# STU filters of a two-layer network: the lower left quarter of the Toeplitz matrix from three block products, and one product for the even and the odd lags of the same source tokens

## The chip, the cores and the metric

The kernel runs on one core of one Trainium2 chip. The metric is the device time of that core in microseconds (us), from the first to the last instruction of one execution of the whole program. The kernel before takes 2966.78 us (median of three runs, 2966.41 to 2967.76). The engines are named as in the profile: PE is TensorE's matrix multiply, PEld its weight load, DVE is VectorE, ACT is ScalarE, POOL is GpSimd, SP the engine that issues most DMAs.

## The reference, cut to what matters

The input is x (8 images, 128 channels, 32 x 32 positions, fp32). Layer 0 is multi-head attention along rows and then a spectral filter unit (STU); layer 1 is a deformable 1 x 3 convolution and a mixture of experts. Each part has a normalisation ahead of it and a residual sum around it. The change is in the STU, whose tokens are the 1024 positions of an image:

```python
Vf = jnp.fft.rfft(phi, n=n, axis=0)                     # 16 filters
Uf_p = jnp.fft.rfft(u, n=n, axis=1)
Uf_m = jnp.fft.rfft(u * sgn3, n=n, axis=1)              # signs + - + - ...
U_plus = jnp.fft.irfft(Vf[None, :, :, None] * Uf_p[:, :, None, :], n=n, axis=1)[:, :sl]
U_minus = jnp.fft.irfft(Vf[None, :, :, None] * Uf_m[:, :, None, :], n=n, axis=1)[:, :sl]
U_minus = U_minus * sgn[None, :, None, None]
out = jnp.einsum('btkd,k,kde->bte', U_plus, s, Mpp)
out = out + jnp.einsum('btkd,k,kde->bte', U_minus, s, Mpm)
```

This is a causal convolution of the tokens u with each of 16 filters, once plain and once with alternating signs, followed by a 128 x 128 matrix for each filter and sign, summed over the filters. The unit is run on the first 1024, 512, 256 and 128 tokens with four sets of matrices, and the four results are mixed with the weights of a softmax. Three more matrices M_u act on the tokens at lags 0, 1 and 2.

## The kernel before

**Even and odd lags.** The sum and the difference of the plain and the signed convolution are the even and the odd lags of the filter. So the kernel splits the tokens into even and odd ones (parity, 512 of each). An output parity gets the even lags from source tokens of the same parity (term 0) and the odd lags from the other parity (term 1). Each of these is a lower triangular Toeplitz matrix of 512 x 512. A filter lies in SBUF as one tile `teto` of 128 partitions: row p holds the filter reversed and shifted, so that any 128 columns of it are one 128 x 128 Toeplitz block. `read_filter` (L1179) loads it with two DMAs, even lags and odd lags.

**One pass.** The images go in four pairs; the list of work is (pair, filter), 4 x 16 = 64 passes. For a pass, `filter_image` (L1367) is called for each of four (parity, term) and each of two images: four matmuls, whose weights are the four token tiles of 128 tokens and whose moving operands are 512, 384, 256 and 128 columns of the filter, add into one PSUM bank `pu` (128 channels x 512 tokens), and ScalarE copies it to `us` (L1378). fp32 products appear as two records each in the profile. `pu` has two banks in rotation. `mix` (L1380) multiplies the `us` of the pass before, for both images, with this filter's mixing matrices `mf`, in four column ranges (SPANS: 64, 64, 128 and 256 tokens, since the four lengths of the STU end at different tokens), and adds into four PSUM banks `po` that stay open for the whole pair. `start_sums` (L1335) opens these banks with the residual and the lags 0 to 2. In program order a filter product of an image (eight records) is followed by half of a mixing step (three short ranges or the long one), and then by other work.

**The other work.** The second layer of the pair before, and the normalisation of the pair to come, are Python generators in a queue `behind`. `advance(2.6)` (L1411) takes steps from it until their costs add up to 2.6; it is called eight times in a pass, after each half of a mixing step. So the order of instructions on each engine is written out by the program. The steps of an image are: transposes, normalisation (`norm_steps`, L779: statistics and scaling on VectorE, Newton steps for the inverse root on GpSimd), a product `p_g` for each tile of 128 tokens, 24 DMAs from SP that write the tables `tab`, offsets, 24 gathers by GpSimd (`fetch`, L1054, three ahead, from a ring of nine buffers `g`) each with four VectorE steps (L1078), a second normalisation, gates, and 16 expert products `p_e` with four VectorE steps each (L1102). The last pair's second layer runs after the spectral stage, two images interleaved.

**Filters and matrices.** At the start of pass n the filter of pass n+2 is loaded (L1436, three buffers), at its end the matrices for pass n+2 (L1460, three buffers). In the first pair `load_matrices` (L1260) loads M_plus and M_minus, GpSimd makes their sum and difference (L1274, L1275), VectorE scales and adds them to `mf` (L1279, L1281), and SP stores `mf` in DRAM (L1284); the other pairs load it from there (L1267). `lags` (L1242) makes `mu` from M_u on VectorE once, before the first pass.

Of the kernel before, what the change touches and what calls it, by code (L numbers as in the profile page):

```python
# [18 lines left out]
P = 128  # L19
B = 8  # L20
C = 128
# [11 lines left out]
PHI_PAD = 127  # L33
PHI_ROW = PHI_PAD + 1 + HT
GROUPS = ((0, 1), (2, 3), (4, 5), (6, 7))
RATE = (2.6, 3.5)
STAGGER = 16


# [361 lines left out]
class BoundedAttention:  # L401
# [6 lines left out]
    def __init__(self, nc, cp):  # L408
        self.nc = nc
        HG, NH = self.HG, self.NH  # L410
        self.xc = cp.tile([P, T], F32, name="xc")
        self.ht = cp.tile([P, NT, C], F32, name="ht")
        self.hk = cp.tile([P, 2 * HT + 2], F32, name="hk")
        self.wq = cp.tile([C, HG, NH, 32], F32, name="wq")
        self.wk = cp.tile([C, HG, NH, 32], F32, name="wk")
        self.wv = cp.tile([C, C], F32, name="wv")
        self.group = cp.tile([P, NG], F32, name="group")
        self.spread = cp.tile([P, 2, P], F32, name="spread")
        self.pick = cp.tile([P, HG, NH, HD], F32, name="pick")
# [381 lines left out]
class DeformAndExperts:  # L801
# [182 lines left out]
    def image(self, b, x2, alone):  # L984
# [69 lines left out]
        def fetch():  # L1054
            if len(fetched) < len(points):
                i, tap = points[len(fetched)]
                if alone:
                    at = idx[:, i, tap : tap + 1]
                else:
                    if tap == 0:  # L1060
                        here.append(sb.tile([P, TAPS], I32, tag="here", name="here", bufs=3))
                        nc.scalar.copy(here[-1], idx[:, i, :])  # L1062
                    at = here[-1][:, tap : tap + 1]
                g = sb.tile([P, 4 * C], F32, tag="g", name="g", bufs=9)
                nc.gpsimd.indirect_dma_start(  # L1065
                    out=g, out_offset=None, in_=rows,
                    in_offset=bass.IndirectOffsetOnAxis(ap=at, axis=0),
                )
                fetched.append(g)
# [106 lines left out]
        yield  # L1176


def read_filter(nc, t, phi_e, phi_o, k):  # L1179
    nc.sync.dma_start(t[:, 0:HT], bass.AP(phi_e.tensor, k * PHI_ROW, [[1, P], [1, HT]]))  # L1180
    nc.sync.dma_start(
        t[:, HT : 2 * HT + 1], bass.AP(phi_o.tensor, k * PHI_ROW, [[1, P], [1, HT + 1]])
    )
    return t[:, 0:HT], t[:, HT : 2 * HT + 1]


class FirstGroup:
# [30 lines left out]
class Spectral:  # L1218
# [4 lines left out]
    def __init__(self, ctx, tc, dram, phi_e, phi_o, M_u, M_plus, M_minus, coef, x1d, back, given):  # L1223
        nc = self.nc = tc.nc
        cp = ctx.enter_context(tc.tile_pool(name="s_const", bufs=1))
        self.sb = ctx.enter_context(tc.tile_pool(name="s_sb", bufs=1))
        self.up = ctx.enter_context(tc.tile_pool(name="s_u", bufs=2, space=PSUM))
        self.op = ctx.enter_context(tc.tile_pool(name="s_o", bufs=1, space=PSUM))
        self.phi_e, self.phi_o, self.x1d, self.back = phi_e, phi_o, x1d, back
        self.M_u, self.M_plus, self.M_minus, self.coef = M_u, M_plus, M_minus, coef  # L1230
# [23 lines left out]
    def load_filter(self, k):  # L1254


        t = self.sb.tile([P, 2 * HT + 1], F32, tag="teto", name="teto", bufs=3)
        return read_filter(self.nc, t, self.phi_e, self.phi_o, k)

    def load_matrices(self, k, first):  # L1260

        nc, sb = self.nc, self.sb
        mf = sb.tile([C, NFR, 2, C], F32, tag="mf", name="mf", bufs=3)
        if not first:
            nc.sync.dma_start(mf, self.mfd[k])  # L1267
            return mf
# [18 lines left out]
    def prepare(self, group):  # L1287

        nc, sb = self.nc, self.sb
        group["x1"], group["ur"] = [], []  # L1290
        for n, b in enumerate(group["images"]):
            x1 = sb.tile([P, NT, C], F32, tag="x1", name="x1", bufs=2)
            nc.gpsimd.indirect_dma_start(
                out=x1.rearrange("p i c -> p (i c)"), out_offset=None,
                in_=self.x1d.rearrange("b p i c -> (b p) (i c)"),
                in_offset=bass.IndirectOffsetOnAxis(ap=self.back[:, b : b + 1], axis=0),
            )
            group["x1"].append(x1)
            if group["number"] % 2:
                group["ur"].append(sb.tile([P, NT, C], F32, tag="ur", name="ur", bufs=2))  # L1300
            else:
                group["ur"].append(self.given.ur[n])
        group["ut"] = sb.tile([C, 2, 2, HT + 1], F32, tag="ut", name="ut")

    def normal(self, group, newton):

        for x1, ur in zip(group["x1"], group["ur"]):
            yield from norm_steps(self.nc, self.sb, x1, ur, 1e-5, newton)

    def channels(self, group, bank):  # L1310

# [52 lines left out]
        )  # L1364
        group["opened"].add(bank)

    def filter_image(self, group, n, par, term, teto, us):  # L1367

        nc = self.nc
        src = par if term == 0 else 1 - par  # L1370
        flt = teto[0] if term == 0 else teto[1][:, par : par + HT]
        pu = self.up.tile([P, HT], F32, tag="u", name="pu")
        for i in range(4):
            nc.tensor.matmul(  # L1374
                pu[:, i * P : HT], group["ur"][n][:, src * 4 + i, :], flt[:, 0 : HT - i * P],
                start=(i == 0), stop=(i == 3),
            )
        nc.scalar.copy(us[:, n, :], pu)  # L1378

    def mix(self, group, par, term, spans, mf, us, last):  # L1380
        for lo, hi, k in spans:
            self.add(
                group, (par, lo // 256), self.span(group, par, lo, hi), mf[:, k - 1, term, :],
                us[:, 0 : len(group["images"]), lo:hi], last and term == 1,
            )

    def finish(self, group):
# [9 lines left out]
def spectral_and_second_layer(tc, spec, layer, weights):  # L1397
    groups = [{"images": im, "number": g} for g, im in enumerate(GROUPS)]
    work = [(g, k) for g in range(len(groups)) for k in range(NF)]
    spec.prepare(groups[0])  # L1400
    filters = {0: spec.given.filter, 1: spec.load_filter(1)}
    matrices = {0: spec.load_matrices(0, True)}
    spec.lags(weights)
    matrices[1] = spec.load_matrices(1, True)


    behind = deque([spec.channels(groups[0], layer.bank), layer.setup()])
# [14 lines left out]
    for n in range(len(work) + 1):  # L1422
# [9 lines left out]
        if now is not None and now[1] == 0 and now[0]:  # L1432
            for _ in starts[now[0]]:
                pass
        if n + 2 < len(work):
            filters[n + 2] = spec.load_filter(work[n + 2][1])  # L1436
        sums = {}
        for i in range(4 if now or before else 0):
            par, term = divmod(i, 2)
            if now is not None:  # L1440
                group = groups[now[0]]
                us = spec.sb.tile([C, 2, HT], F32, tag="us", name="us", bufs=6)
                sums[i] = us
            for m in range(2):
                unit = now is not None and m < len(group["images"])
                if unit:
                    spec.filter_image(group, m, par, term, filters[n], us)
                if before is not None:
                    if before[1] == 0 and i + m == 0:
                        spec.start_sums(groups[before[0]])  # L1450
                    spec.mix(
                        groups[before[0]], par, term, SPANS[0:3] if m == 0 else SPANS[3:4],
                        matrices[n - 1], kept[i], before[1] == NF - 1,
                    )
                if unit:
                    advance(RATE[2 - len(group["images"])])
        if before is not None and before[1] == NF - 1:
            spec.finish(groups[before[0]])
        if n + 2 < len(work):
            matrices[n + 2] = spec.load_matrices(work[n + 2][1], work[n + 2][0] == 0)  # L1460
        kept, before = sums, now
    while behind:
        advance(1)
# [105 lines left out]
```

## Time and profile before

| | |
|---|---|
| median of three runs | 2966.78 us |
| the profiled execution | 2968.47 us, its span 2966.7 us |
| attention, to the first filter product | 0 to 911 us |
| first pair, passes 0 to 15 | 911 to 1331 us |
| second, third and fourth pair | 1331 to 1803, 2275 and 2745 us |
| second layer of the last pair | 2745 to 2967 us |
| filter products in the profile | 4096 records |
| copies `us` (L1378) | 512 of 585 ns |
| combining steps `mf` (L1279, L1281) | 16 of 354 ns and 48 of 485 ns |
| sums and differences `both` (L1274, L1275) | 32 of some 1265 ns |

A row of the timeline holds start, length, engine, line, operation, output and input names, shape and count of one or several like instructions; in brackets stands the idle time of the engine before it and what ended that. A matmul's record lasts longer than the time to the next one's start, since they are pipelined; work on TensorE is therefore counted from start to start. In a table by windows each engine has its busy time and, in brackets, its count of instructions; the granted TensorE clock (1.00 is full), the share of the DMA engines and GB/s end the row.

### The profile page before, as it was taken

Reading aid. Unit: us, or ns where it says so; the run is one execution under the profiler, and the core shown is the slowest. Engines: PE = TensorE matmul, PEld = TensorE weight load, DVE = VectorE, ACT = ScalarE, POOL = GpSimd, SP = SyncE. Lnnn points to the kernel's source line nnn. Section 1 sums busy time; section 2 is a strip of 40 time slices with the busy share of each in tenths; the row PEclk is TensorE's granted clock in tenths of the full one; section 3 lists DMA queues with packets and bytes.
Section 4 is the critical chain, followed back from the end, with each engine's and each line's share of the span. In section 5 each row is a group of like instructions: output and inputs, shape, how many; then the busy total and the mean of one; then the engine's idle time right before and its main releaser. Section 6 shows DMA issues by size and latency. Waiting matters only on the chain.

```text
span 2966.7 us, 45298 instructions
## 1 busy us (share of the span) xinstructions
PE 2759.9 (93%) x18896; PEld 1693.4 (57%) x18896; DVE 1405.6 (47%) x2882; ACT 982.0 (33%) x1246; POOL 976.3 (33%) x977
## 2 busy tenths in 40 slices
PE   7999999999998999999999999999999999999316
PEld 3555555555555666666666666666666666666103
DVE  4888888888882200000432532333333153333586
ACT  4666667676661111112212111221211221221100
POOL 4777777777881211100200301210210030220230
PEclk9999999999998999999999999999999999999658
DMA  1000000000002322221614411521621441530730
GB/s 27 2 16 16 2 16 16 2 16 9 16 16 83 101 64 64 64 61 51 184 39 128 143 35 36 170 82 41 191 64 36 116 135 34 157 99 8 229 112 15
DMA packets 177012, 199.80 MB, mean 67 GB/s; under 512 B 17237, under 2 KB 135189, under 8 KB 176801
## 3 DMA queue, kind: packets, MB, share of 16 engines
q1 hardware_dynamic: 147328, 134.97, 15.3%
q0 software_dynamic: 16800, 55.59, 6.1%
q10 hardware_dynamic: 12672, 6.29, 0.7%
q8 instruction: 150, 2.46, 0.3%
q14 instruction: 62, 0.50, 0.1%
HBM read 128.88 MB, written 67.92 MB: 66 GB/s over the span
## 4 chain that ended last, share of the span: by engine, by line
PE 58%; DVE 6%; DMA 1%; issue 1%; POOL 0%; ACT 0%; SPq 0%; DVEq 0%; POOLq 0%; ACTq 0%
PE pu L1374 35%; PE po L1362 16%; PE p_e L1096 3%; DVE x L1078 2%; PE p_g L1015 1%; DVE x L1102 1%; DMA tab<-gs 1%; PE p_out L1113 0%; PE p_turn L918 0%; PE p_out L1116 0%; PE p_l L1140 0%; DVE st L785 0%; DVE mv L786 0%; PE p_ut L1318 0%; DMA g<-tab,cn_idx 0%
## 5 line engine op out<-in xcount | busy, mean ns | idle before, releaser
L1378 ACT COPY us<-pu 128x512 f32<-128x512 f32 x512 | 299.4, 585 | 1301.1 <-PE pu L1374 1266.9
L620 POOL TENSOR_TENSOR t<-e 128x1024 f32<-128x1024 f32 x256 | 607.9, 2375 | 199.4 <-ACT e L611 199.2
L648 DVE TENSOR_TENSOR e<-e,rb 128x2048 f32<-128x2048 f32 x256 | 570.8, 2279 | 83.6 <-PE rb L641 83.6
L1374 PE MATMUL pu<-teto,ur 128*128 128x512 f32 (+3 forms) x2048 | 594.4, 433 | 0.0
L611 ACT ACTIVATE e<-s 128x2048 f32<-128x2048 f32 x256 | 480.9, 1879 | 253.2 <-PE s L606 251.3
L1374 PEld LDWEIGHTS pu<-teto,ur 128*128 128x128 f32 x2048 | 386.5, 190 | 273.0 <-issue 185.1
L1362 PE MATMUL po<-us,mf 128*128 128x128 f32 (+2 forms) x2048 | 528.1, 381 | 0.0
L606 PE MATMUL s<-q,k 32*128 32x256 f32 x4096 | 296.1, 403 | 14.0 <-ACT e L611 13.2
L658 PE MATMUL av<-e,vt 128*32 128x256 f32 x4096 | 290.0, 391 | 2.9 <-DVE e L648 1.6
L1374 PE MATMUL pu<-teto,xc 128*128 128x512 f32 x992 | 290.5, 436 | 0.0
L1374 PE MATMUL pu<-teto,ht 128*128 128x512 f32 x992 | 287.7, 433 | 0.0
L1065 POOL DMA_INDIRECT g<-tab,here x144 | 137.6, 956 | 447.0 <-ACT here L1062 252.8
L1374 PEld LDWEIGHTS pu<-teto,xc 128*128 128x128 f32 x992 | 189.0, 191 | 153.9 <-issue 114.2
L1362 PEld LDWEIGHTS po<-us,mf 128*128 128x128 f32 x2048 | 270.9, 192 | 4.1 <-issue 3.9
L1078 DVE SCALAR_TENSOR_TENSOR x<-g,w,x 128x128 f32<-128x128 f32 x704 | 250.0, 356 | 43.0 <-DMA g<-tab,here 11.5
L1102 DVE SCALAR_TENSOR_TENSOR x<-p_e,gates,x 128x128 f32<-128x128 f32 x512 | 177.7, 350 | 188.7 <-PE p_e L1096 172.4
L606 PEld LDWEIGHTS s<-q,k 32*128 32x128 f32 x4096 | 186.4, 185 | 136.9 <-ACT e L611 115.7
L1374 PEld LDWEIGHTS pu<-teto,ht 128*128 128x128 f32 x992 | 187.7, 190 | 110.0 <-issue 64.7
L770 POOL TENSOR_SCALAR rs_v<-rs_v 128x8 f32<-128x8 f32 x18 | 4.4, 245 | 711.3 <-DVE rs_b L768 711.3
L658 PEld LDWEIGHTS av<-e,vt 128*32 128x32 f32 x4096 | 101.7, 109 | 141.4 <-issue 85.2
L1096 PE MATMUL p_e<-ew,tc 128*128 128x512 f32 x256 | 133.1, 626 | 15.4 <-DVE x L1102 10.3
L634 DVE RECIPROCAL r<-z 128x256 f32<-128x256 f32 x64 | 112.5, 1757 | 69.0 <-PE z L627 68.8
(237 smaller groups left out, 1829.0 us busy)
## 6 DMA issues: line engine op xcount, KB each, us to landing
tab<-gs SPq DMA_DIRECT2D x168, 256.0 KB
mf<-mfd SPq DMA_DIRECT2D x48, 512.0 KB
teto<-in_phi_o SPq DMA_DIRECT2D x63, 256.5 KB
teto<-in_phi_e SPq DMA_DIRECT2D x63, 256.0 KB
mfd<-mf SPq DMA_DIRECT2D x16, 512.0 KB
tab<-gs ACTq DMA_DIRECT2D x24, 256.0 KB
xc<-in_x SPq DMA_DIRECT2D x8, 512.0 KB
x1d<-xt SPq DMA_DIRECT2D x8, 512.0 KB
```

Of the source, the lines that this page charges most:

```text
L606: nc.tensor.matmul(s[:, j, c, :], img["k"][rows, hg, 2 * r + c, :], q[rows, qc * QU : (qc + 1) * QU], start=True, stop=True,)
L611: nc.scalar.activation(e.rearrange("p j c q -> p (j c q)"), s.rearrange("p j c q -> p (j c q)"), AF.Exp, scale=float(HD) ** -0.5,)
L620: nc.gpsimd.tensor_add(t, e[:, :, 0, :], e[:, :, 1, :])
L648: nc.vector.tensor_tensor(e, e, un["rb"].unsqueeze(2).to_broadcast([P, NH, 2, QU]), ALU.mult)
L658: nc.tensor.matmul(qrt["av"][32 * j : 32 * j + 32, 0:QU], img["v"][:, 2 * r + c, P * hg + 32 * j : P * hg + 32 * j + 32], un["e", r][:, j, ...
L1065: nc.gpsimd.indirect_dma_start(out=g, out_offset=None, in_=rows, in_offset=bass.IndirectOffsetOnAxis(ap=at, axis=0),)
L1078: nc.vector.scalar_tensor_tensor(x3[:, i, :], fetched[n][:, k * C : (k + 1) * C], w[:, i, tap, k : k + 1], (tok if tap + k == 0 else x3)[: ...
L1096: nc.tensor.matmul(pe, tc[:, i * P : (i + 1) * P], self.ew[:, grp * 4 : grp * 4 + 4, :].rearrange("d e c -> d (e c)"), start=True, stop=True,)
L1102: nc.vector.scalar_tensor_tensor(x3[:, i, :], pe[:, k * C : (k + 1) * C], gate[:, i, grp * 4 + k : grp * 4 + k + 1], x3[:, i, :], ALU.mult ...
L1362: self.nc.tensor.matmul(out, lhsT, rhs, start=bank not in group["opened"], stop=last, skip_group_check=True)
L1374: nc.tensor.matmul(pu[:, i * P : HT], group["ur"][n][:, src * 4 + i, :], flt[:, 0 : HT - i * P], start=(i == 0), stop=(i == 3),)
L1378: nc.scalar.copy(us[:, n, :], pu)
```

## The change

A 512 x 512 Toeplitz matrix has four rows and columns of 128 x 128 blocks T0 (diagonal) to T3. The lower left quarter takes tiles 0 and 1 to output blocks 2 and 3 and needs T2 t0 + T1 t1 and T3 t0 + T2 t1. The kernel after forms W = T2 (t0 + t1) once and adds (T1 - T2) t1 and (T3 - T2) t0: three block products for four. The sums t0 + t1 (`add_tiles`) are made by VectorE once for each image and parity, the differences of blocks (`differences`) by GpSimd once for each pass, for the even and the odd lags.

A product now has both kinds of lags in its moving operand, as two halves of the columns, since both act on the same source tokens. So a unit is (image, source parity), four in a pass. It has seven products: W (2 x 128 columns) in the bank `low`; 2 x 256 and three times 256 columns in the bank `high`; 512 and 256 columns in the bank `low` again. ScalarE copies W out of PSUM, VectorE adds W to the high half on its way to `us`, ScalarE copies the low half. Each of the two banks has one buffer.

```diff
-RATE = (2.6, 3.5)
+RATE = 2.6
...
-                g = sb.tile([P, 4 * C], F32, tag="g", name="g", bufs=9)
+                g = sb.tile([P, 4 * C], F32, tag="g", name="g", bufs=7)
...
-        self.up = ctx.enter_context(tc.tile_pool(name="s_u", bufs=2, space=PSUM))
+        self.up = ctx.enter_context(tc.tile_pool(name="s_u", bufs=1, space=PSUM))
...
-        t = self.sb.tile([P, 2 * HT + 1], F32, tag="teto", name="teto", bufs=3)
-        return read_filter(self.nc, t, self.phi_e, self.phi_o, k)
+        return read_filter(
+            self.nc, self.sb.tile([P, FILTER], F32, tag="teto", name="teto", bufs=2),
+            self.phi_e, self.phi_o, k,
+        )
+
+    def differences(self, t):
+        nc = self.nc
+        d = self.sb.tile([P, 5 * DIFF], F32, tag="diff", name="diff", bufs=2)
+        for lags, width in enumerate((P, P + 1)):
+            at = HT * lags
+            nc.gpsimd.tensor_sub(
+                d[:, DIFF * lags : DIFF * lags + 4 * DIFF].rearrange(
+                    "p (two c) -> p two c", two=2
+                )[:, :, 0:width],
+                t[:, at + P : at + 5 * P].rearrange("p (two c) -> p two c", two=2)[:, :, 0:width],
+                t[:, at + 2 * P : at + 2 * P + width].unsqueeze(1).to_broadcast([P, 2, width]),
+            )
+        return d
...
-        mf = sb.tile([C, NFR, 2, C], F32, tag="mf", name="mf", bufs=3)
+        mf = sb.tile([C, NFR, 2, C], F32, tag="mf", name="mf", bufs=2)
...
+        self.add_tiles(group)
+        yield
+
+    def add_tiles(self, group):
+        for ur, both in zip(group["ur"], group["sum"]):
+            halves = ur.rearrange("p (par i) c -> p par i c", par=2)
+            self.nc.vector.tensor_add(both, halves[:, :, 0, :], halves[:, :, 1, :])
...
+        pw = bank("low")[:, :, 0:P]
+        product(pw, group["sum"][n][:, src, :], blocks(2 * P, 3 * P), True, True)
+        w = self.sb.tile([C, 2, P], F32, tag="us_w", name="us_w", bufs=2)
+        nc.scalar.copy(w, pw)
+        tile = [ur[:, src * 4 + i, :] for i in range(4)]
+        high = bank("high")
+        product(high, tile[2], blocks(0, 2 * P), True)
+        product(high[:, :, 0:P], tile[1], less(0))
+        product(high[:, :, P:], tile[0], less(1))
+        product(high[:, :, P:], tile[3], blocks(0, P), False, True)
+        nc.vector.tensor_tensor(
+            us[:, :, n, 2 * P :].rearrange("c two (b t) -> c two b t", b=2),
+            high.rearrange("c two (b t) -> c two b t", b=2),
+            w.unsqueeze(2).to_broadcast([C, 2, 2, P]), ALU.add,
+        )
+        low = bank("low")
+        product(low, tile[0], blocks(0, 2 * P), True)
+        product(low[:, :, P:], tile[1], blocks(0, P), False, True)
+        nc.scalar.copy(us[:, :, n, 0 : 2 * P], low)
...
+    less = {0: spec.differences(filters[0])}
+    spec.add_tiles(groups[0])
     matrices = {0: spec.load_matrices(0, True)}
     spec.lags(weights)
-    matrices[1] = spec.load_matrices(1, True)
...
-        if n + 2 < len(work):
-            filters[n + 2] = spec.load_filter(work[n + 2][1])
...
+                    spec.filter_image(group, m, src, filters[n], less[n], us)
+                    if src + m == 0 and n + 1 < len(work):
+                        less[n + 1] = spec.differences(filters[n + 1])
+
+                for part in (SPANS[0:3], SPANS[3:4]):
+                    if before is not None:
...
+                            matrices[n - 1], kept[src], before[1] == NF - 1,
+                        )
+                    if now is not None:
+                        advance(RATE)
...
         if n + 2 < len(work):
-            matrices[n + 2] = spec.load_matrices(work[n + 2][1], work[n + 2][0] == 0)
+            filters[n + 2] = spec.load_filter(work[n + 2][1])
+        if n + 1 < len(work):
+            matrices[n + 1] = spec.load_matrices(work[n + 1][1], work[n + 1][0] == 0)
```

After a unit both halves of a mixing step follow, each with an `advance(2.6)`, so there are still eight in a pass. The filter of pass n+2 is loaded at the end of pass n (two buffers instead of three) and the matrices for pass n+1 right after it (two instead of three, one pass ahead instead of two). The differences for pass n+1 are issued in pass n after its first unit. The ring of gather buffers has seven instead of nine. `add_tiles` adds one step to the normalisation of a pair. Before, the matrices of filter 1 were made ahead of the first pass; now they are made at its end.

## The prediction

> **What bounds the kernel now.** First the page's busy shares and its forty slices. They show two stages: attention, and from slice 13 a stage in which TensorE is busy without a break.
>
> ```profile
> PE 2759.9 (93%) x18896; PEld 1693.4 (57%) x18896; DVE 1405.6 (47%) x2882; ACT 982.0 (33%) x1246; POOL 976.3 (33%) x977
> ...
> PE   7999999999998999999999999999999999999316
> ...
> PE pu L1374 35%; PE po L1362 16%; PE p_e L1096 3%; DVE x L1078 2%; PE p_g L1015 1%; DVE x L1102 1%; DMA tab<-gs 1%; PE p_out L1113 0%; PE p_turn L918 0%; PE p_out L1116 0%; PE p_l L1140 0%; DVE st L785 0%; DVE mv L786 0%; PE p_ut L1318 0%; DMA g<-tab,cn_idx 0%
> ```
>
> The last line is the chain that ended last: filter products (pu) hold 35% of the span. Second, busy time by window, one row per stretch (us, busy us and count by engine, clock, DMA):
>
> ```profile
> 1016.20:1331.00 314.80, 314.80 (x1250) 204.43 (x1249) 21.70 (x48) 60.85 (x104) 27.36 (x22) 1.00 0.22 62
> 1331.00:1803.00 472.00, 463.88 (x1902) 302.81 (x1901) 163.75 (x570) 97.30 (x187) 69.20 (x133) 0.99 0.32 96
> ```
>
> TensorE never rests in passes 3 to 15 (first row: 13 passes, 24.2 us each) and is 98% busy in the second group, where VectorE works 35% of the time. So TensorE work removed here is time saved, unless something else ends last. The timeline of TensorE gives the price:
>
> ```profile
> 1318.88 2.32 PE L1374 MATMUL pu<-teto,xc 128*128 128x512 f32 x8
> 1321.04 1.04 PE L1362 MATMUL po<-us,mf 128*128 128x128 f32 x6
> 1321.92 2.32 PE L1374 MATMUL pu<-teto,ht 128*128 128x512 f32 x8
> 1324.08 1.02 PE L1362 MATMUL po<-us,mf 128*128 128x512 f32 x2
> ```
>
> Start to start, eight records (four products, 512+384+256+128 = 1280 columns) take 2.16 us, 1.69 ns a column; the mixing halves take 0.88 and 0.86.
>
> [...] after 6.2 us of idle at 1793.5 sixteen records took 3.54 us, start to next start, for about 1.8. [...]
>
> **The change, part by part.** *Products.* A unit (image, source parity) makes 256 (W) + 1280 (high) + 768 (low) = 2304 columns, 3.89 us. A pass has four: 15.55 us against 8 x 2.16 = 17.28. Saved: 1.73 us x 64 = **-110.6 us**.
>
> *Added on idle engines.* The combine, 256 times 128x512 on VectorE, reads PSUM. Its nearest row is the division e<-e,rb, also a tensor_tensor with a broadcast: 2279 ns for 2048 elements. [...] for 512 an estimate of 0.69 us (bounds 0.65 and 0.8). 256 x 0.69 = 177 us over 1.8 ms of a third-busy engine: nothing by load. ScalarE gets 256 copies of 585 ns and 256 of some 366 (the 128x256 row) for 512 of 585. The differences on GpSimd (128 at about 0.74, by its 128x256 row) are made a pass ahead. All cost nothing as load; what they add is *order*: TensorE's next high products wait for the previous unit's combine (one bank), and that combine stands in VectorE's queue behind whatever was issued earlier. Cover after a high part: low 1.29, mixing 1.74, next W 0.43 = 3.5 us.
>
> *Where that cover fails: the first image pair, passes 2 to 15.* Here each pass makes the next mixing matrix from M_plus and M_minus. Before, nothing urgent stood behind it. Filter load, matrix loads, GpSimd and VectorE in one such pass:
>
> ```profile
> 1067.24 0.42 SPq L1180 DMA_DIRECT2D teto<-in_phi_e  x1
> 1067.71 0.78 SPq L1181 DMA_DIRECT2D teto<-in_phi_o  x1
> 1068.63 0.38 SPq L1271 DMA_DIRECT2D mp<-in_M_plus  x1
> 1069.11 0.44 SPq L1272 DMA_DIRECT2D mm<-in_M_minus  x1
> ...
> 1074.80 1.26 POOL L1274 TENSOR_TENSOR both<-mp,mm 128x512 f32<-128x512 f32 x1 [21.36 <-DMA mm<-in_M_minus]
> 1076.02 1.26 POOL L1275 TENSOR_TENSOR both<-mp,mm 128x512 f32<-128x512 f32 x1
> ...
> 1089.12 0.35 DVE L1279 TENSOR_SCALAR mf<-both,coef 128x256 f32<-128x256 f32 x1 [22.30 <-PE po L1362]
> 1089.51 1.53 DVE L1281 SCALAR_TENSOR_TENSOR mf<-both,coef,mf 128x256 f32<-128x256 f32 x3
> ```
>
> With two filter buffers the load of filter n+2 waits for the last low product of pass n, and the loads of matrix n+1 now stand behind it on SP. The matrix steps stand in VectorE's queue ahead of the first combine of pass n+1. From the last low product: drain and SP 0.2; 1 MB lands 6.3 later (before, 1.5 MB took 7.6 from the filter's issue, and 0.5 MB alone took 4.4 at 939.7; bounds 5.8 and 7.0); GpSimd 2.5; matrix 1.9; combine 0.7; semaphores 0.1: 11.7. TensorE meanwhile has mixing 1.74, a unit 3.89, mixing 1.74, W 0.43 = 7.8. Idle **3.9 us** (3.2 to 4.7). [...] 14 x 6.1 = **+85.4**. These passes should take 28.6 us, not 24.2. Pass 2 also held 7.5 us of waits for the second pair's normalisation (35.2 us less 24.2 and 3.5 of p_ut); they now lie under this stall: **-7.5**.
>
> *Start.* The first combine stands behind mu (L1250), whose last step ran at 941.98. Before, TensorE went through pass 0 by 934.9. Now unit 1 waits until 943.4, restarts at half speed (+2.7), ends pass 0 near 959 and pass 1 near 996.7 instead of 981.06: 15.6, or **+19.1** before the two passes' saving. Differences and sums at the start lie under this wait. In pass 1 the opening sums (15 us of TensorE) cover the matrix.
>
> *Passes 16 to 63.* Matrices are only loaded, so that wait is gone. Steps of the second layer now come in pairs 0.9 us apart, then none for 4.8, where they were 3.0 apart. Chains such as statistics, GpSimd's 3.5 us of Newton steps, normalisation, transpose, and the gates, lose about 2.3 us an image: +14. At the first gather VectorE now holds TensorE:
>
> ```profile
> 1431.64 0.35 DVE L1078 SCALAR_TENSOR_TENSOR x<-g,w,tok 128x128 f32<-128x128 f32 x1 [9.09 <-DMA g<-tab,here]
> ```
>
> Its step was issued near 1426.4 (by ScalarE's copies), 5 us earlier; the table writes (22 in 20.24 us on SP) bound it. With the combine queued behind it I get 2.2 us an image and 1 for the clock: 6 x 3.2 = +19. Together **+33**. Seven gather buffers for nine: two interleaved images need seven live, so nothing; at worst 2 us in the tail. Matrices in two buffers still have a whole pass to load: nothing.
>
> **Sum:** -110.6 + 85.4 - 7.5 + 19.1 + 33 = **+19.4**. The profiled execution took 2968.5 (span 2966.7), 1.7 over the median 2966.8; set on the median: **2986 us**.
>
> **Rivals.** *The stall comes, but short or warm (faster).* If the clock does not fall, the 14 passes cost 54.6 and the sum is -11: 2955. It decides at 4.7 us of stall and clock together per pass; I have 6.1. For it: at 939.1 TensorE idled 3.6 us without an immediate drop. Against: two microseconds more did drop it[...]. *The chain is covered* (loads early enough, combine not delayed): -66, 2901. Against: 11.7 us of measured pieces facing 7.8. *VectorE's queue also blocks the later passes*: each second-layer chain costs twice or more, one microsecond more in each of 48 passes: 3034. For it: VectorE now sits between TensorE and TensorE throughout; against: gathers leave it 1.7 us free in every 5.6 us unit. *The products do not get cheaper* because of split operands (two runs of 128 or 256): against it, the mixing's 128x2x64 forms keep the price per column.
>
> **How the numbers follow.** Forecast, 2972 to 3010: 0.53. Short or warm stall, 2940 to 2972: 0.22. Covered: 0.06. Blocked later: 0.19. The range 2944 to 3026 leaves out the covered case and two thirds of the last. About 0.2% (6 us) is what a measurement of this kernel tells from no change: below 2961 lie the covered case and 0.17 of the second: faster 0.23; same 0.13, the rest of it and the forecast's edge; slower 0.64.
>
> **What would show it.** Right: filter products near 995 us of TensorE work for 1106; in the first pair, passes of 28 to 29 us, with TensorE idle some 4 us before a high product, released by VectorE, whose combine follows the matrix steps, and a clock of 0.9 there; pass 0 ending near 959; from pass 16 on, passes shorter by 1.5. Wrong: passes of 22.5 us in the first pair (loads earlier than I think), or TensorE idle beside VectorE in the gathers.

## The result and the profile after

The changed kernel takes **3055.7 us** (median of four runs, 3053.7 to 3059.0) against 2967.3 us (2966.4 to 2968.9) for the kernel before on the same chip: ratio 1.030, 95% interval 1.028 to 1.032. It is 88 us slower; the forecast was 19 us slower. The profiled execution took 3059.0 us (span 3057.3), so the stages below differ from those of the execution before (span 2966.7) by 90.6 us in all.

The page of the changed kernel: busy shares, the forty slices, the granted clock, and the chain that ended last by line.

```profile
PE 2719.0 (89%) x18384; PEld 1702.4 (56%) x18384; DVE 1592.9 (52%) x3146; ACT 926.0 (30%) x1246; POOL 1070.8 (35%) x1105
...
PE   7999999999977888889999898999898999999416
...
PEclk9999999999998989899999999999999999999658
...
PE pu_high L1422 17%; PE po L1393 13%; PE pu_low L1422 12%; PE s L606 9%; PE av L658 8%; PE z L627 3%; PE p_e L1096 3%; SPq L1008 3%; DMA mm<-in_M_minus 3%; PE rb L641 2%; DVE x L1078 2%; ACT e L611 1%; DVE x L1102 1%; PE pk L575 1%; PE pq 
```

There are 256 matrix products fewer (512 records), but TensorE is busy for only 41 us less, and slices 13 to 18, most of the passes of the first image pair, show 7 and 8 tenths where they showed 8 and 9, with the clock at 8 and 9 tenths in turn. In the chain, matrix loads (DMA mm) and table writes (SPq L1008) have come in with 3% each.

Busy time by window (us, busy us and count by engine, granted clock, DMA share, GB/s): passes 3 to 15 of the first pair, and the second pair from its opening sums to those of the next.

```profile
1031.50:1422.86 391.36, 328.69 (x1145) 217.70 (x1144) 68.53 (x104) 49.78 (x104) 50.66 (x52) 0.90 0.18 52
1449.38:1923.96 474.58, 445.69 (x1776) 301.83 (x1776) 209.22 (x636) 83.82 (x188) 93.09 (x165) 0.97 0.32 94
```

The 13 passes take 30.1 us each, where they took 24.2, and TensorE rests a sixth of that time. The second pair takes 474.6 us for 472.8, although its products are 27.7 us cheaper.

Divided by stages, each from its first product or opening sum to the next (us):

| stage | before | after | measured | forecast |
|---|---|---|---|---|
| attention to the first product of pass 2 | 981.1 | 997.9 | +16.8 | +15.6 |
| passes 2 to 15 | 349.9 | 425.0 | +75.0 | +53.7 |
| pass 16 to the end of the last filter product | 1404.5 | 1403.4 | -1.2 | -50 |
| tail | 231.2 | 231.1 | -0.2 | 0 |

The start came as forecast. Two terms missed: 21 us in the first pair, and 49 us in the three later pairs, where the whole gain was eaten.

**One pass of the first pair.** The timeline of the changed kernel, from the end of one pass into the next (start, duration, engine, operation; in brackets the idle time before it and what ended it):

```profile
1090.97 0.34 SPq L1184 DMA_DIRECT2D teto<-in_phi_e  x1
...
1092.46 0.59 PE L1422 MATMUL pu_low<-teto,sum 128*128 128x256 f32 x2
...
1096.34 1.90 PE L1393 MATMUL po<-us,mf 128*128 128x128 f32 x8
...
1097.74 1.26 POOL L1296 TENSOR_TENSOR both<-mp,mm 128x512 f32<-128x512 f32 x1 [26.13 <-DMA mm<-in_M_minus]
...
1098.96 1.26 POOL L1297 TENSOR_TENSOR both<-mp,mm 128x512 f32<-128x512 f32 x1
1100.18 1.46 POOL L1273 TENSOR_TENSOR diff<-teto 128x256 f32<-128x256 f32 x2
1100.26 0.80 DVE L1301 TENSOR_SCALAR mf<-both,coef 128x256 f32<-128x256 f32 x1 [9.86 <-POOL both L1297]
1101.09 1.87 DVE L1303 SCALAR_TENSOR_TENSOR mf<-both,coef,mf 128x256 f32<-128x256 f32 x3
1102.88 0.68 DVE L1434 TENSOR_TENSOR us<-pu_high,us_w 128x512 f32<-128x512 f32 x1
...
1103.62 2.08 PE L1422 MATMUL pu_high<-teto,ht 128*128 128x512 f32 x2 [4.95 <-DVE us L1434]
```

This is the chain that the prediction drew: loads, GpSimd, matrix steps, combine, high product. A unit (1092.46 to the mixing at 1096.34) takes 3.88 us, as computed. But mp and mm land 6.8 us after the filter's issue (6.7 on average over the 14 passes) rather than 6.3; the matrix steps take 2.7 us rather than 1.9; and the two 512-column records after the wait take 2.08 us instead of 1.02, at a granted clock of 0.50. VectorE kept to the order of its queue: the combine's data were there when the high products ended, at 1095.2, but it ran at 1102.88, after the four steps that could not start before 1100.26.

**The second gather of a pair.** SyncE, GpSimd, VectorE and TensorE of the changed kernel, in the second pair:

```profile
1698.88 12.34 SPq L1008 DMA_DIRECT2D tab<-gs  x13
1711.34 0.80 SPq L1184 DMA_DIRECT2D teto<-in_phi_e  x1
...
1716.71 0.72 POOL L1273 TENSOR_TENSOR diff<-teto 128x256 f32<-128x256 f32 x1 [37.93 <-DMA teto<-in_phi_e]
...
1720.83 1.05 POOL L1065 DMA_INDIRECT g<-tab,here  x1 [0.15 <-issue]
...
1724.43 0.35 DVE L1078 SCALAR_TENSOR_TENSOR x<-g,w,tok 128x128 f32<-128x128 f32 x1 [12.80 <-DMA g<-tab,here]
1724.82 1.13 DVE L1078 SCALAR_TENSOR_TENSOR x<-g,w,x 128x128 f32<-128x128 f32 x3
1725.86 0.68 DVE L1434 TENSOR_TENSOR us<-pu_high,us_w 128x512 f32<-128x512 f32 x1
...
1726.60 2.07 PE L1422 MATMUL pu_high<-teto,ur 128*128 128x512 f32 x2 [9.74 <-DVE us L1434]
```

Table writes hold up the filter load, that load holds up the differences, and the gather stands behind them in GpSimd's queue. The first gather step waits at the head of VectorE's queue, the combine behind it, and TensorE behind the combine. That is 9.7 us, then eight high records in 4.10 us, start to next start, for 2.15. The first image's gather costs 3.75 us in the same way (1522.32). The later pairs also wait 3.3 us for the gates instead of 1.2, and 5.6 us for a normalisation ahead of p_ut that did not show before. Together 3.75 + 9.74 + 2.1 + 5.6 = 21.2 us more waits in this pair; the pair is 29.5 us over 472.8 - 27.7. The other 8.3 us are about what the half clock takes: the granted clock was 0.50 in two microseconds right after three of these waits (from 1522.3, 1726.6 and 1883.7) and from 1 us after the start of the fourth's work (1819.4), and the four passes are 1.9 to 2.5 us longer than the added wait alone explains.

### The profile page after: what moved, and what is told of

Its sections match the earlier page's. It is cut to its first block, busy times and chain, and to the rows that moved or that the text cites. A ratio compares the mean times of both kernels' runs of the same rounds, so it can differ in the third digit from the quotient of the medians.

```text
span 3057.3 us, 45004 instructions
## 1 busy us (share of the span) xinstructions
PE 2719.0 (89%) x18384; PEld 1702.4 (56%) x18384; DVE 1592.9 (52%) x3146; ACT 926.0 (30%) x1246; POOL 1070.8 (35%) x1105
## 4 chain that ended last, share of the span: by engine, by line
PE 75%; DVE 7%; DMA 6%; SPq 4%; issue 3%; POOL 2%; ACT 2%; POOLq 0%; DVEq 0%; ACTq 0%
PE pu_high L1422 17%; PE po L1393 13%; PE pu_low L1422 12%; PE s L606 9%; PE av L658 8%; PE z L627 3%; PE p_e L1096 3%; SPq L1008 3%; DMA mm<-in_M_minus 3%; PE rb L641 2%; DVE x L1078 2%; ACT e L611 1%; DVE x L1102 1%; PE pk L575 1%; PE pq L561 1%
## 5 line engine op out<-in xcount | busy, mean ns | idle before, releaser
L1434 DVE TENSOR_TENSOR us<-pu_high,us_w 128x512 f32<-128x512 f32 x256 | 176.8, 691 | 658.7 <-PE pu_high L1422 658.7
L1393 PE MATMUL po<-us,mf 128*128 128x128 f32 (+2 forms) x2048 | 496.5, 381 | 0.0
L1442 ACT COPY us<-pu_low 128x512 f32<-128x512 f32 x256 | 149.8, 585 | 969.1 <-PE pu_low L1422 969.1
L1393 PEld LDWEIGHTS po<-us,mf 128*128 128x128 f32 x2048 | 307.3, 191 | 44.6 <-issue 21.9
L1273 POOL TENSOR_TENSOR diff<-teto 128x256 f32<-128x256 f32 x126 | 92.2, 744 | 661.9 <-DMA teto<-in_phi_e 557.1
L1422 PE MATMUL pu_high<-teto,ur 128*128 128x512 f32 (+1 forms) x512 | 212.8, 498 | 27.2 <-DVE us L1434 27.2
L1427 ACT COPY us_w<-pu_low 128x256 f32<-128x256 f32 x256 | 95.4, 373 | 419.6 <-PE pu_low L1422 360.3
L1422 PE MATMUL pu_low<-teto,ur 128*128 128x512 f32 (+1 forms) x512 | 187.0, 487 | 0.0
L1422 PE MATMUL pu_high<-teto,ht 128*128 128x512 f32 x248 | 121.9, 578 | 71.9 <-DVE us L1434 71.9
L1422 PEld LDWEIGHTS pu_low<-teto,sum 128*128 128x128 f32 x504 | 94.2, 191 | 107.6 <-issue 105.4
```

The lines of the kernel that those rows point to most:

```text
L1393: self.nc.tensor.matmul(out, lhsT, rhs, start=bank not in group["opened"], stop=last, skip_group_check=True)
L1422: nc.tensor.matmul(out, weights, moving, start=start, stop=stop, skip_group_check=True)
L1434: nc.vector.tensor_tensor(us[:, :, n, 2 * P :].rearrange("c two (b t) -> c two b t", b=2), high.rearrange("c two (b t) -> c two b t", b=2) ...
L1442: nc.scalar.copy(us[:, :, n, 0 : 2 * P], low)
```

## The experiments

All times are medians, and all ratios go against the kernel before on the same chip. Its own median was between 2965.3 and 2969.8 on the three chips used, so differences between kernels measured on different chips are good to some 4 us.

| kernel | us | ratio (95% interval) |
|---|---|---|
| matrix steps later | 2947.5 | 0.992 (0.991 to 0.994) |
| matrix loads first | 2956.6 | 0.996 (0.994 to 0.997) |
| differences later | 3026.9 | 1.019 (1.018 to 1.021) |
| no combine | 2883.5 | 0.971 (0.969 to 0.973) |
| before, with the new loads | 2958.1 | 0.997 (0.996 to 0.999) |
| both orders | 2924.9 | 0.986 (0.984 to 0.988) |
| + gather step later | 2916.7 | 0.983 (0.981 to 0.985) |
| + lag steps spread | 2912.2 | 0.982 (0.980 to 0.983) |
| + start free | 2902.5 | 0.978 (0.977 to 0.980) |
| + room in the plan | 2885.3 | 0.972 (0.971 to 0.974) |

The theory: TensorE's products got cheaper as computed, and everything lost is order, that is, a combine standing in VectorE's queue behind a step whose data are late. The rivals: late loads or smaller buffers cost by themselves, or the new products are dearer than their columns.

**Matrix steps later.** The steps are split off load_matrices and issued in the next pass.

```diff
+        self.late = partial(self.matrix_steps, mf, both, k)
         return mf
...
+                    if src == 1 and m == 0 and spec.late:
+                        spec.late()
```

> One edit to the changed kernel: the four VectorE steps that make the mixing matrix of pass n+2 are issued after the third unit of pass n+1, no longer ahead of its first combine. Loads, buffers and products are as in the changed kernel. Theory (the stall of the first pair is the order of VectorE's queue: the combine stands behind matrix steps that wait for loads): TensorE's waits for the combine in passes 3 to 15 fall from 4.7 us a pass to nothing, the clock there goes back to 1.0, passes take 22.5 us instead of 30.3, pass 2 gets back some 7.5 us of waits for the second pair's normalisation; 95 us less than the changed kernel, 2960 us (2948 to 2975). The later pairs stay as they are. Rival (two filter buffers make the loads late, and something needs the loaded data itself): the wait moves to the mixing or the next filter and the time stays within 20 us of 3056.

Measured 2947.5 us, 108 less than the changed kernel. The same 13 passes by window:

```profile
1022.21:1313.97 291.76, 291.76 (x1145) 200.75 (x1144) 58.27 (x104) 49.88 (x104) 50.25 (x52) 1.00 0.23 70
```

Passes of 22.4 us, TensorE never idle, clock 1.00: the loads are as late as before (6.5 us after the filter's issue on average), and only the place of the matrix steps in VectorE's queue differs, and with it that of the store of their result in SyncE's. The rival falls. Of the 13 us beyond the expectation 7.5 are the normalisation waits of pass 2, which did not come back (26.1 us, of which the 3.7 over the others are p_ut's own work); the rest was not traced. The later pairs stayed at 475.7 and 474.5 us. The steps also took 0.34 and 0.485 us each here, away from GpSimd's work, so VectorE's busy time in the window fell by 10.3 us, 0.8 a pass.

**Matrix loads first.** The two statements at the end of a pass change places.

```diff
-        if n + 2 < len(work):
-            filters[n + 2] = spec.load_filter(work[n + 2][1])
         if n + 1 < len(work):
             matrices[n + 1] = spec.load_matrices(work[n + 1][1], work[n + 1][0] == 0)
+        if n + 2 < len(work):
+            filters[n + 2] = spec.load_filter(work[n + 2][1])
```

> One edit to the changed kernel: at the end of a pass SyncE issues the matrix loads ahead of the filter load instead of behind it. Theory (queue order): the chain loads, GpSimd, matrix steps, combine starts with 0.5 MB that lands after some 4.4 us instead of 6.8, so each wait of 4.7 us in the first pair shrinks by about 2.3 us and the loss of clock by about as large a share; passes of 26.5 to 28 us instead of 30.3, 3010 us (2995 to 3025). A small step in the loads moves the wait by that step, as a chain would. Rival (the wait comes from elsewhere, and the loads are not on the path): no change, 3056.

Measured 2956.6 us: 99 less, not 46. Passes 3 to 15 take 22.4 us without a wait here too. The direction was right, the size was not, and the timeline of this run says why:

```profile
1094.69 0.42 SPq L1184 DMA_DIRECT2D teto<-in_phi_e  x1
...
1096.05 0.39 SPq L1293 DMA_DIRECT2D mp<-in_M_plus  x1
...
1103.24 1.27 POOL L1296 TENSOR_TENSOR both<-mp,mm 128x512 f32<-128x512 f32 x1 [0.95 <-DMA mm<-in_M_minus]
...
1114.80 0.35 DVE L1301 TENSOR_SCALAR mf<-both,coef 128x256 f32<-128x256 f32 x1 [2.33 <-PE po L1393]
```

The matrix loads here do not wait for the end of their pass. They are issued as soon as the filter load ahead of them is, a whole pass earlier, since their own buffers are long free; the matrix steps then wait only for the mixing to release the matrix buffer (PE po), at the pass's end. What had made them late was the filter load waiting for its buffer at the head of SyncE's queue. I had priced a shift of the landing and missed that the queue would run ahead.

**Differences later.**

```diff
-                    if src + m == 0 and n + 1 < len(work):
+                    if src == 1 and m == 0 and n + 1 < len(work):
```

> One edit to the changed kernel: the differences of the next filter are made on GpSimd after the third unit of a pass instead of after the first, so that GpSimd no longer works beside the matrix steps of VectorE. Theory (VectorE and GpSimd slow each other down): the four matrix steps take 1.9 us as in the kernel before, not 2.7; each wait of the first pair shrinks by 0.8 us and a little clock, 14 times about 1.1 us: 3040 us (3030 to 3050). Rival (the steps are slow for another reason, such as loads arriving at the same time): 2.7 us as before and 3056.

Measured 3026.9 us, 29 less, but mostly not for the reason given. In 13 of the 16 passes that make a matrix GpSimd had nothing else to do, so the differences still ran at once beside the matrix steps, which stayed at 0.80 and 1.87 us. In the other three they ran apart from them, and the steps took their old time, as in the one ahead of pass 2's wait:

```profile
1003.07 0.35 DVE L1301 TENSOR_SCALAR mf<-both,coef 128x256 f32<-128x256 f32 x1 [3.30 <-POOL both L1297]
1003.46 1.53 DVE L1303 SCALAR_TENSOR_TENSOR mf<-both,coef,mf 128x256 f32<-128x256 f32 x3
```

There TensorE waited 3.8 us instead of 5.1. So within this run the steps take 1.9 us without GpSimd's subtractions beside them and 2.7 with them, as the theory has it. Most of the gain, some 22 us, is in the later pairs, 466.2 and 467.8 us for 474.6 and 474.9 in the first two: the gathers are now ahead of the differences in GpSimd's queue, and the pass of the second gather takes 28.9 us instead of 34.3. In the first pair passes fell by 0.4 us; 0.25 of it is loads that landed sooner on average (6.5 us after the filter's issue for 6.7), and why they did is open.

**No combine.** W is not added in; the high half is only copied.

```diff
-        nc.vector.tensor_tensor(
-            us[:, :, n, 2 * P :].rearrange("c two (b t) -> c two b t", b=2),
-            high.rearrange("c two (b t) -> c two b t", b=2),
-            w.unsqueeze(2).to_broadcast([C, 2, 2, P]), ALU.add,
-        )
+        nc.scalar.copy(us[:, :, n, 2 * P :], high)
```

> One edit to the changed kernel: the VectorE combine is replaced by a plain ScalarE copy of the high bank, so nothing that TensorE waits for stands in VectorE's queue any more. The contribution of W to the high half is left out; all TensorE products, loads, differences and matrix steps remain. It measures what the products save by themselves. Theory (everything lost is order in VectorE's queue): passes of 22.5 us throughout, no wait of a high product for more than a fraction of a microsecond, clock 0.99: 110 us of products less than the kernel before, plus 5 us of a later start: 2862 us (2850 to 2885). Rival (the products or the clock are dearer than their columns): above 2920.

Measured 2883.5 us, 172 less than the changed kernel and 21 more than expected. Passes 3 to 15 take 22.4 us and no high product waits. The surplus is in the later pairs, 457.3 us where 445.1 was possible:

```profile
1325.58:1782.91 457.33, 441.81 (x1776) 299.42 (x1775) 167.27 (x572) 121.51 (x252) 93.53 (x166) 0.99 0.33 97
```

TensorE waits 3.3 us for the gates (1.2 before), 1.1 and 7.7 ahead of p_ut (6.2 before), and 3.4 in the pass after the second gather, where ScalarE copied the high bank after 5.3 us of idle time, whose end the profile does not name:

```profile
1605.49 0.58 ACT L1434 COPY us<-pu_high 128x512 f32<-128x512 f32 x1 [5.34 <-remote]
```

That pass takes 27.7 us here and the full-speed 22.4 in the changed kernel, so some 5 of the 12 us are this run's own. The other 7 us a pair the second layer's chains lose even where VectorE holds nothing up. That the new rhythm of their steps is the cause is argued; no run changed the rhythm alone. The remaining 22 us of the changed kernel's loss of 29.5 a pair come with the combine: the two passes of its first gathers are 5.6 and 11.9 us longer than here, and the pass of its normalisation 4.5.

**The kernel before, with the new loads and buffers.**

```diff
-        mf = sb.tile([C, NFR, 2, C], F32, tag="mf", name="mf", bufs=3)
+        mf = sb.tile([C, NFR, 2, C], F32, tag="mf", name="mf", bufs=2)
...
+        if n + 1 < len(work):
+            matrices[n + 1] = spec.load_matrices(work[n + 1][1], work[n + 1][0] == 0)
```

> The kernel before, with its eight products per image and its copies on ScalarE, but with the buffers and the loads of the changed one: two filter buffers and two matrix buffers, seven gather buffers, the filter of pass n+2 and the matrix of pass n+1 loaded at the end of pass n. Theory (late loads cost nothing unless a combine that TensorE waits for stands behind them in VectorE's queue): passes of 24.2 us without a wait in the first pair, and the time of the kernel before within 6 us: 2967 us. Rival (smaller buffers and late loads are the cost by themselves): 40 us slower or more.

Measured 2958.1 us, 7 less than the kernel before beside it:

```profile
981.00:1022.00 41.00, 41.00 (x180) 27.77 (x179) 11.32 (x43) 9.38 (x16) 10.18 (x30) 1.00 0.29 77
1022.00:1331.00 309.00, 309.00 (x1226) 200.63 (x1226) 21.69 (x48) 59.77 (x102) 29.87 (x24) 1.00 0.23 65
```

Late loads and fewer buffers cost nothing where no combine stands behind them. The normalisation waits of pass 2 are gone as well; which of the load and buffer edits removed them was not separated.

**Both orders.** Matrix steps after the second unit and differences after the third.

```diff
-                    if src + m == 0 and n + 1 < len(work):
+                    if src == 0 and m == 1 and spec.late:
+                        spec.late()
+                    if src == 1 and m == 0 and n + 1 < len(work):
```

> The changed kernel with the matrix steps on VectorE issued after the second unit of the next pass, and the differences on GpSimd after its third. Theory: the first pair keeps the 22.4 us of the run with late steps; in the later pairs the pass of the second gather, 34.7 us there, falls to about 29, because the gathers no longer stand in GpSimd's queue behind differences that wait for a filter load behind 24 table writes. About 8 us a pair, 24 less than with late steps alone: 2924 us (2915 to 2933). Rival (the second gather waits for the table writes only): 2947.

Measured 2924.9 us, as expected. Around the second gather:

```profile
1601.90 1.05 POOL L1065 DMA_INDIRECT g<-tab,here  x1 [33.75 <-DMA teto<-in_phi_e]
...
1606.31 0.35 DVE L1078 SCALAR_TENSOR_TENSOR x<-g,w,tok 128x128 f32<-128x128 f32 x1 [7.61 <-DMA g<-tab,here]
...
1608.48 2.08 PE L1428 MATMUL pu_high<-teto,ur 128*128 128x512 f32 x2 [4.54 <-DVE us L1440]
1609.26 1.58 POOL L1273 TENSOR_TENSOR diff<-teto 128x256 f32<-128x256 f32 x2
```

The differences come after the gathers, and TensorE's wait falls from 9.6 us to 4.5. GpSimd's queue was half of the second gather's cost; the rest is the gather step issued ahead of its rows.

**Gather step later.**

```diff
-RATE = 2.6
+RATE = 2.8
...
         yield
-        yield
+        yield 1.0 if alone else 11.4
```

> As the run before (both orders mended), and the first gather step of each of the six interleaved images is issued some 10 us later in the plan (a pause of 11.4 planned microseconds instead of 1), with 2.8 instead of 2.6 planned us of second-layer work after each part, so that the work of an image still ends within its pair. Theory (TensorE's waits left in the later pairs are combines that stand behind a first gather step issued before its rows have landed): the passes of the first gathers fall to about 22.5 us, waits for the combine in the later pairs from some 9 us a pair to nearly nothing, 2898 us (2888 to 2912). Rival (the wait is only handed on, to gates, transposes or the next pair's normalisation): above 2915.

Measured 2916.7 us: the rival's side of the line. The waits for the combine in the later pairs are gone, as the theory has it, but only 8 of the expected 27 us came in: the first image's gates now keep TensorE waiting 4.1 us too, and the passes around them take 31.3 and 37.3 us where they took 26.7 and 35.5. That the denser plan causes this, and not the pause, was not tried apart.

**Lag steps spread.**

```diff
-    spec.late()
-    spec.lags(weights)
+    lags = spec.lags(weights)
...
+                    if n == 0:
+                        next(lags, None)
```

> As the run before, and the four steps on VectorE that make the lag matrices mu are issued one after each of the four units of pass 0 instead of all ahead of its combines; the matrix of pass 0 is made after its second unit. Theory (the wait of 16 to 18 us at the start is the first combine standing behind mu in VectorE's queue): the wait is gone, pass 0 takes some 24 us instead of 45 as in the run without a combine, and some 6 of the 21 us come back as waits for the second pair's normalisation in pass 2: 15 us less than the run before (10 to 21). Rival (the data come too late for pass 1 anyhow): no gain.

Measured 2912.2 us, 4.5 less instead of 15. The wait at the start fell from 14.9 us to 9.1: the lag loads now stood behind weight loads on SyncE, and one combine behind an addition that waits for a bias load.

**Start free.** The lag loads go together and first, the addition late.

```diff
+        for f in range(NFR):
+            nc.sync.dma_start(loads[:, f], self.M_u[f].rearrange("i d e -> d i e"))
...
-        nc.vector.tensor_tensor(
-            self.base, self.base, bias.unsqueeze(1).to_broadcast([P, NT, 9]), ALU.add
-        )
```

> As the run with the lag steps spread, and two further things are taken out of the way of the combines of pass 0: the four lag loads are issued together ahead of the layer's weight loads (into a us buffer that pass 0 does not use), and the VectorE addition that waits for a bias load is issued at the end of the layer's setup. Theory (what was left of the wait at the start, 9.1 us, is one combine behind that addition and the lag loads behind weight loads on SyncE): no wait above 2 us after the first high product, pass 0 takes 24 to 26 us instead of 36, of which some 5 come back as waits in pass 2; 2905 us (2901 to 2911). Rival (pass 1 waits for mu instead): 2912.

Measured 2902.5 us, as expected. Pass 0 takes 24.6 us for 45.0 in the changed kernel, with no wait above 1.1 us after its first product.

**Room in the plan.**

```diff
-RATE = 2.8
+RATE = 3.2
...
         yield
-        yield
+        yield 8.0
         pgt = self.bank("p_gt")
...
         yield
-        yield
+        yield 6.0
         yield from self.channels(group, bank)
```

> As the run before, with room in the plan of the second layer where TensorE still waited: a pause of 8 planned us instead of 1 ahead of the transposition of the gates, 6 instead of 1 ahead of the transpositions that open the next pair, and 3.2 instead of 2.8 planned us of work after each part, with which all of a pair's work is issued before the pair ends (with 2.8 some 20 steps are issued at once at its end). Theory (the waits for gates, 4.1 and 3.3 us a pair, and for the normalisation, 5.5 and 6.3, are the same kind of cost as the first gathers, steps issued sooner than their data): they go, with the half clock after them; 45 us less than the run before, 2860 us (2845 to 2880). Rival (denser steps put new waits elsewhere): above 2890.

Measured 2885.3 us, 17 less, between the two. The waits for gates and normalisation in the interleaved part are gone, but one of 4.6 us in pass 2 came in, and one of 4.7 to 5.2 at the first gather of each of the three interleaved pairs:

```profile
1393.50 1.07 POOL L1065 DMA_INDIRECT g<-tab,here  x1 [35.51 <-ACT us_w L1439]
...
1397.11 1.41 POOL L1279 TENSOR_TENSOR diff<-teto 128x256 f32<-128x256 f32 x2
1398.58 1.65 PE L1434 MATMUL pu_high<-diff,ur 128*128 128x256 f32 x3 [4.70 <-POOL diff L1279]
```

Now the differences stand behind the gathers, and TensorE waits 4.7 us for them. With all products of the changed kernel, this version is 2.8% faster than the kernel before, with the interval above.

## Why the prediction was right and wrong

The direction was right, the size was not. Two terms of the sum were too small: the stall of the first pair, +85 for a measured +107, and passes 16 to 63, +33 for a measured +82.

*Products:* right. A unit takes 3.88 us for 3.89; passes without a wait take 22.44 us for 24.2, 1.77 a pass for 1.73. The rival of dearer products is out.

*Combine:* right, 691 ns for 0.69 us, which was the author's estimate. The kernel before has a row of the same size: VectorE's eight copies of 128x512 out of PSUM (x<-po, L1394) took 692 ns.

*First-pair stall:* the mechanism was right, and the matrix-steps run shows it by moving those steps alone. The size was 7.7 us a pass, not 6.1: idle 4.84 on average over 14 waits (3.87 to 6.28) for 3.9, just above its bounds of 3.2 to 4.7, and 2.8 of clock for 2.2. That 2.2, the rest of the 6.1, was the author's estimate; no trace of before shows it. The idle time missed on the landing (6.7 for 6.3) and on the matrix steps (2.7 for 1.9). The steps' price was taken from a row where GpSimd was idle; here its differences ran at the same time. The first step took 0.80 us for 0.35 beside GpSimd's subtractions, in the run with later differences too, and 0.35 in its three passes in which they ran apart. Why the steps are slower there no run shows.

*Pass 2's old waits, -7.5:* these were 3.6 us of idle time and the half clock after it (0.50 from 1006 to 1012 us of the kernel before, where eight records took 4.26 us for 2.16). They did go, but not only because they "lie under this stall": with the stall gone and the wait at the start kept (matrix steps later) they stayed away. The run without a combine has neither of the two, and there 4.5 us of waiting for p_ut were back in pass 2 (32.5 us). So the start's wait may have covered them; but the kernel before lost them with the new loads alone, and which of these counts in the changed kernel stays open.

*Start, +19.1 gross:* right in place and size; before the two passes' saving, 16.8 + 3.5 = 20.3. After the wait of 16.08 us the eight high records took 3.85 us for 2.15, so the half clock cost 1.7 there; the forecast's 2.7 was the author's estimate. The last two runs on the start show what it consisted of. The sums hold the first product back to 916.28 for 911.18; that lay under the wait, as the prediction had it, and shows only when the wait is gone: with the start freed, the first product still waits 5.3 us for them.

*Passes 16 to 63, +33:* wrong, and this is the largest error: it measured about +82 (-1.2 + 83). The step that failed is "All cost nothing as load; what they add is *order*": for the differences on GpSimd the prediction stopped at the load, and followed order in VectorE's queue alone. GpSimd's queue holds the gathers too, and its differences wait for a filter load behind the table writes. Summed over the six passes of first gathers, each against the same pass of the kernel before less the measured saving of 1.77 us, this part measured 57 us for a forecast of 19 (6 x 3.2). With the differences alone moved it was 32: so 25 of the 38 us missed were GpSimd's order. The other 13 are the price of a gather step issued ahead of its rows, which was set at 3.2 us for every image alike, 1 of it for the clock, the author's estimate; in the changed kernel the first cost 3.75 of wait and the second 9.74, and the half clock 1.7 and 1.95 us more in the eight records after them. The chains' +14 was small as well: the remaining passes lost 27 us, and still some 21 without a combine, that run's own waits for ScalarE left out.

The rival *VectorE's queue also blocks the later passes* gave one microsecond in each of 48 passes and 3034 us. Its sum for these passes was nearly exact, 48 us for 49, and that is luck: its "twice or more" for each chain was near, but 25 of the gathers' 57 us came from GpSimd's queue, of which it does not speak, and the loss falls on 11 passes with waits, while the others are within 1 us of their price. I held against it that gathers leave VectorE 1.7 us free in each unit. That is about right (17.2 of 28 us busy after the second gather) and beside the point, since the waits come from the data of the first step, not from VectorE's load.

*Short or warm stall, covered chain:* out. The clock fell to half in each of passes 2 to 15 (the two 512-column records after each wait took 2.07 or 2.08 us for 1.02; 0.90 in the window), and the chain was longer than the cover. In the kernel before, the granted clock was 1.00 from 940 to 944 us, across the end of an idle stretch of 3.64 us; with 2.08 us more of idle time it was 0.94 from 944 to 948 and 0.63 from 948 to 952.

*Buffers (g, mf): nothing:* right, by the run of the kernel before with these buffers.

## What to carry to other kernels

When an edit puts an engine between two steps of the bound engine, its queue becomes part of the critical path (VectorE ran the combine at 1102.88, though its data were there at 1095.2, behind steps that waited until 1100.26): walk through everything that is issued ahead of the new step on that engine and ask what each waits for, and do the same for every queue that feeds it, DMA issue and GpSimd included. A cheaper product that adds such a step wants its neighbours re-ordered at the same time; here two statements that changed places were worth 99 us, and four VectorE steps issued later 108. And look for a load at the head of a DMA queue that waits for a buffer: here it kept back the matrix loads behind it, which went a pass of 22.4 us sooner once the two had changed places.

## What the runs showed of the hardware

- VectorE slowed beside GpSimd: the first matrix step took 0.80 us instead of 0.34 to 0.35, the first of the other three 0.83 instead of 0.485, when two GpSimd subtractions of 0.74 us ran at the same time; within the run with later differences both times occur, 13 passes with the subtractions beside and three without.
- An idle stretch of 4.84 us in every pass of 30 us cost some 2.8 us more in half clock (granted 0.50 from 1103.6 to 1106.4 us and 0.62 from there to 1110.0), so that the wait's price was 1.6 times its length. After the waits of 3.75 and 9.74 us, eight records of 2.15 us took 3.84 and 4.10.
- In the run with the matrix loads first, these loads, whose buffers were free, were issued a whole pass of 22.4 us sooner, right behind the filter load of one pass earlier in SyncE's queue (filter at 1094.69, mp at 1096.05).
